# A graph-attention layer: the edge mask's chain started earlier, its merge moved to k steps 0 and 1, x loaded in whole rows, 12 more filler steps ahead of the scores

## The chip, the cores and the metric

One Trainium2 chip, one core. The metric is the device time of one execution in microseconds (us). The kernel before took 312.18 us (median of 3 runs, 310.19 to 312.44).

## The reference

There are 384 nodes with 1024 features, 16 heads of 64, and 6528 edges of the form (src, dst, type).

```python
h = jnp.maximum(_layernorm(x, axis=-1), 0.0)
q, k, v = h @ wq.T + bq, h @ wk.T + bk, h @ wv.T + bv
q2, k2, v2 = q @ wiq.T + biq, k @ wik.T + bik, v @ wiv.T + biv     # each split into 16 heads
w = softplus(edge_type_weights)
mask = full((384, 384), -inf); mask = mask.at[src, dst].set(w[edge_type - 1])
mask[i, i] = w[3] where the diagonal is still -inf
attn = softmax(q2 @ k2.T / 8 + mask)
out = x + (attn @ v2) @ wo.T + bo
```

Seven 1024x1024 weights are read, and the mask is a scatter of 6528 values into 384x384 cells, in which the last edge of a cell wins. All of it is in float32.

## The kernel before, in words

**Matmuls.** Each operand is split into a high and a low part in the matmul type fp32r (`split_hi`, L67, on ScalarE; `split_lo`, L79, on VectorE or GpSimd), and each product is three matmuls: high by high, high by low, low by high (L357 to L359). A weight comes in 8 chunks of 128x1024 (512 KB), loaded by SP (L65) into three `raw` buffers and split into four `whl` buffers.

**Stages.** The chunks are numbered w: 8 of v, 8 of q, 8 of v2 (`iv`), 8 of k, then 8 pairs of q2 and k2 (`iq`, `ik`), then 8 of the output. In the v, q and k stages (`proj`, L394) chunk m gives 128 rows of the transposed result in a PSUM bank `g`, 24 matmuls of 384 columns. At the head of each chunk (`slot_head`, L385) come the split of chunk w+2, the evacuation of the chunk before (`evac_row`, L370: L372 on VectorE scales by the row of 1/std and writes `f`, L373 on ScalarE makes the high part, L374 on VectorE the low one), and the load of chunk w+4. The order on every engine is the program's order, written by hand; every engine works strictly through it. The v2 stage (L492) has 18 matmuls of 512 columns a chunk and sums into six PSUM banks, one of them a `g` bank. They are evacuated one per chunk in the k stage (`v2_evac`, L503), the one in `g` last, so `g` has two banks for the k stage until then.

**Scores.** From L727 on, 48 steps (16 heads by 3 row tiles) do the scores, the softmax, the transposes and the product with v2. Between them a filler of q2/k2 chunks and then of output chunks is issued (`fill`, L712): `PRE` matmuls ahead of the first scores and `RATE` per step. Scores add the mask `ma` (L660).

**The mask.** `er` holds the edges with 128 per row, `ed` the same edges with 128 per column. `key_rows_a` and `key_rows_b` (L173, L177) make keys src*384+dst on GpSimd and write them to `krow` in DRAM; `key_load(g)` (L188) broadcasts a third of the rows to all partitions (3 DMAs of 384 KB). For each of 51 columns `mask_detect` (L204, VectorE) counts whether a later edge of the column has the same key; `mask_index` (L210) sends such edges to a dump cell. `mask_scatter` (L217) writes a column's 128 values by an indirect DMA from GpSimd into one of three DRAM tables in turn, so that the order between columns is kept by table; a scatter waits for the landing of the one before it in its table. The tables are cleared first (`table_clear`, L142, from `zero`). `val`, the softplus of the edge's type, is made on GpSimd after `softplus_c` (L160); `mask_base` (L197) puts the default on the diagonal of `ma`. At the end `mask_load` (L223) reads the three tables back and `mask_select` (L231, VectorE) merges each into `ma`, in order.

`detect(s)` (L419) places this in slots, one per chunk of v and q (s = 0 to 15): 5 detects a slot from s = 3, 3 scatters a slot from s = 7 and in each v2 chunk; `mask_load` stands at k step 2 and the merges at k steps 5, 6 and 7.

**The start.** x is loaded in six half tiles; statistics on VectorE (L243), the mean's subtraction on ScalarE, GpSimd and VectorE (`ln_sub`), transposes on TensorE (L284), high parts on ScalarE (L290), low parts on VectorE (L295). Then chunk 0's 24 matmuls (L402). `residual(k)` (L470), in the v2 stage, adds `bo` to x and keeps the sum in DRAM.

Of the kernel before, what the change touches and what calls it, by code (L numbers as in the profile page):

```python
# [8 lines left out]
F32 = mybir.dt.float32  # L9
# [3 lines left out]
OP = mybir.AluOpType  # L13
# [9 lines left out]
def gnn_kernel(ctx: ExitStack, tc: tile.TileContext, x, edges, erows, etw, wq, wk, wv, wiq, wik, wiv, wo,  # L23
# [15 lines left out]
    EB = 8  # L39
    DS = 3  # L40
    NTAB, RNG = 3, EC // 3
    WARM = (20, 0, 0, 0)

# [49 lines left out]
    for t in range(NT):  # L93
        for c in (slice(0, 512), slice(512, D)):
            nc.sync.dma_start(xt[t][:, c], x[t * 128:(t + 1) * 128, c])
    ert = work.tile([128, N], F32, tag="e", name="er", bufs=EB)
    er = ert[:EC, :256].bitcast(I32).rearrange("p (a j) -> p a j", a=2)
    nc.sync.dma_start(er, erows)
    load(0)
    ed = const.tile([128, 3 * EC], I32, name="ed")  # L100
# [5 lines left out]
    nc.sync.dma_start(ew, etw.partition_broadcast(128))  # L106
    load(2)
# [4 lines left out]
    nc.gpsimd.memset(upper, 1.0)  # L112
    nc.gpsimd.affine_select(upper, upper, pattern=[[1, 128]], compare_op=OP.is_gt, fill=0.0, base=0,
                            channel_multiplier=-1)
    epsc = const.tile([128, 1], F32, name="epsc")
# [17 lines left out]

    def mask_consts():
        nc.gpsimd.iota(dump.bitcast(I32), pattern=[[0, 1]], base=CELLS, channel_multiplier=1)
        nc.gpsimd.tensor_copy(w8[:, 8:9], dump.bitcast(I32))
        nc.gpsimd.memset(zero, 0.0)
        nc.gpsimd.memset(ma, -3.0e38)
        for j in range(NT):
            nc.gpsimd.tensor_scalar(ma[:, j, j * 128:(j + 1) * 128], ident, 3.0e38, -3.0e38, op0=OP.mult, op1=OP.add)  # L140
# [36 lines left out]
    def key_rows_b():  # L177
        nc.gpsimd.tensor_tensor(krt[:EC, :128], kf[:, 0, :], kf[:, 1, :], OP.add)
        nc.gpsimd.dma_start(krow, krt[:EC, :128])

# [6 lines left out]

    def key_load(g):  # L188
        t = work.tile([128, 2, NT, N], F32R, tag="pt", name="rows")
        rv = t.bitcast(F32).rearrange("p a k n -> p (a k n)")  # L190
        for s, (c0, c1) in enumerate(parts(g)):
            dst = rv[:, s * PA * 128:(s * PA + c1 - c0) * 128]
            for c in range(c0, c1):
                rows[c] = rv[:, (s * PA + c - c0) * 128:(s * PA + c - c0 + 1) * 128]
            nc.gpsimd.dma_start(dst, krow[c0:c1, :].rearrange("c j -> (c j)").partition_broadcast(128))

# [12 lines left out]

    def mask_index(cs):  # L210
        t0 = tmpe[:, 0, cs]
        nc.vector.tensor_scalar(t0, key[:, cs], -1.0, w8[:, 8:9], op0=OP.mult, op1=OP.add)
        nc.vector.scalar_tensor_tensor(t0, cnt[:, cs], 0.5, t0, op0=OP.is_gt, op1=OP.mult)
        nc.vector.tensor_tensor(t0, t0, key[:, cs], OP.add)
        nc.vector.tensor_copy(idx[:, cs], t0)

# [85 lines left out]

    mask_consts()
    warm(WARM[0])
    ln_bn(0, 0)
# [7 lines left out]
    p0 = ln_transpose(0)  # L313
    warm(WARM[1])
    ln_sub(1, 0, 512, nc.scalar)
    ln_sub(1, 512, D, nc.gpsimd)
    ln_hi(0, 0, p0[0])
    ln_bn(2, 0)
# [5 lines left out]
    p1 = ln_transpose(1)  # L324
    warm(WARM[2])
    ln_hi(1, 0, p1[0])
    ln_hi(1, 1, p1[1])
    p2 = ln_transpose(2)
    warm(WARM[3])
    t0 = wpool.tile([128, 2, D], F32R, tag="whl", name="whl", bufs=4)  # L330
    whl[0] = (t0[:, 0, :], t0[:, 1, :])
    for c in (slice(0, 512), slice(512, D)):
        nc.vector.tensor_copy(t0[:, 0, c], raw[0][:, c])
    for c in (slice(0, 512), slice(512, D)):
# [59 lines left out]
    def proj(src, dst, bidx, extra=None):  # L394
        nonlocal w
        for m in range(8):
            slot_head(w)
            ps = bank("g")
            if w == 0:
                for i, (a, b) in enumerate(((0, 0), (1, 0), (0, 1))):  # L400
                    for k in range(KT):
                        nc.tensor.matmul(ps[:, :N], whl[0][a][:, k * 128:(k + 1) * 128], src[:, b, k, :],  # L402
                                         start=(i == 0 and k == 0), stop=(i == 2 and k == KT - 1))
# [15 lines left out]
    def detect(s):  # L419

        if s == 0:
            softplus_a()
        if s == 1:
            softplus_b()
        if s == 2:
            softplus_c()
        if s == 2:
            key_load(1)
        if s == 3:
            mask_base()  # L430
        for i in range(max(5 * (s - DS), 0), max(0, min(EC, 5 * (s + 1 - DS)))):
            mask_detect(sc_order[i])
            if i % (NTAB * PA) == NTAB * PA - 1 or i == EC - 1:
                g = i // (NTAB * PA)
                for c0, c1 in parts(g):
                    mask_index(slice(c0, c1))
                if g == 0:
                    key_load(2)
        if s >= DS + 4:
            scatters(3)  # L440
        if s == DS + 11:
            biv_load()

# [48 lines left out]
    for k in range(8):  # L492
# [6 lines left out]
        scatters(3)  # L499
        residual(k)  # L500
        w += 1

    def v2_evac(i):  # L503
# [69 lines left out]
    LT, LA = 5, 7  # L573
    PRE, RATE, RATE_O, RATE_E = 72, 7.9, 8, 8
    WSTEPS = (37, 38, 41, 44, 47, 51)
# [239 lines left out]
```

## Time and profile before

| | us |
|---|---|
| median of 3 runs | 312.18 (310.19 to 312.44) |
| the profiled execution | 312.79 |
| its span, first to last instruction | 311.1 |
| first matmul of chunk 0 (L402) | 12.57 |
| first and last scatter start (L219) | 49.31, 136.56 |
| first merge (L233) | 143.41 |
| first scores (L654) | 168.54 |

The page shares out the span by engine: PE is TensorE's matmuls, PEld its weight loads, DVE VectorE, ACT ScalarE, POOL GpSimd, SP SyncE. Lists of waits name the waiting instruction, whom it waited for, the sum, the number and the longest. A row of the timeline has the start, the duration, engine, line, operation, output and inputs, and in brackets how long the engine sat idle before it and what ended that. Matmuls overlap: a row of 0.33 us follows the last by 0.17. PEclk is the TensorE clock that was granted, in tenths.

### The profile page before, as it was taken

The page shows a single profiled execution, that of the slowest core. Times are in us where ns is not written, and L with a number is a line of the kernel's source. Part 1 is how long each engine was busy: PE and PEld are TensorE (multiplying, and loading weights), DVE is VectorE, ACT ScalarE, POOL GpSimd, SP SyncE. Part 2 cuts the span into 40 slices and gives each one's busy share as a digit, 9 for nine tenths or more (in the row PEclk, how much of TensorE's full clock was granted, in tenths as well). Part 3 has the DMA queues.
Part 4 walks back from the last instruction along what each step waited for, and adds up shares of the span by engine and source line. Part 5 has one row for each costly group of instructions (what it writes and reads, how often), then busy time and mean ns, then how long its engine had stood idle before and what let it go on. Part 6 is the DMA issues. An engine that isn't in the chain of part 4 may idle for free.

```text
span 311.1 us, 4980 instructions
## 1 busy us (share of the span) xinstructions
PE 296.4 (95%) x1643; PEld 280.5 (90%) x1643; DVE 204.4 (66%) x519; ACT 154.2 (50%) x286; POOL 163.0 (52%) x172
## 2 busy tenths in 40 slices
PE   7899999999999999996995999999999999999995
PEld 5799999999888899995994899999999999888884
DVE  3976599999942436864961547576767676896413
ACT  2848242424632126432152477877768686876200
POOL 5655816568756655761033174655647388467010
PEclk9799999999999999998998899999999999999998
DMA  7697868635775776437249586464647477920005
GB/s 226 218 363 267 237 193 212 188 113 176 220 272 161 231 247 208 129 122 250 81 110 265 137 226 174 126 171 118 182 119 187 115 186 241 304 112 0 2 0 202
DMA packets 22031, 55.12 MB, mean 177 GB/s; under 512 B 4598, under 2 KB 8234, under 8 KB 22006
## 3 DMA queue, kind: packets, MB, share of 16 engines
q1 hardware_dynamic: 19190, 49.64, 51.5%
q0 software_dynamic: 2816, 5.17, 6.5%
q8 instruction: 13, 0.21, 0.3%
q14 instruction: 12, 0.10, 0.1%
HBM read 40.39 MB, written 4.97 MB: 146 GB/s over the span
## 4 chain that ended last, share of the span: by engine, by line
PE 45%; DMA 20%; DVE 19%; POOL 7%; issue 4%; ACT 3%; SPq 1%; DVEq 0%; ACTq 0%; POOLq 0%
DMA tab<-val,idx 11%; PE g L359 8%; PE g L357 8%; PE g L358 8%; DVE whl L82 6%; PE s L654 6%; PE a L691 5%; PE t L674 5%; POOL tab L219 5%; DVE junk L207 4%; DVE g L374 3%; DVE f L372 2%; DMA rows<-krow 2%; DMA krow<-kr 2%; DMA ks<-nat 2%
## 5 line engine op out<-in xcount | busy, mean ns | idle before, releaser
L357 PE MATMUL g<-g,whl 128*128 128x384 f32 x312 | 107.8, 346 | 3.1 <-DVE f L372 3.1
L359 PE MATMUL g<-g,whl 128*128 128x384 f32 x312 | 105.8, 339 | 0.4 <-DVE whl L82 0.4
L358 PE MATMUL g<-g,whl 128*128 128x384 f32 x312 | 105.5, 338 | 0.0
L219 POOL DMA_INDIRECT tab<-val,idx x51 | 58.3, 1143 | 30.2 <-DMA tab<-val,idx 16.5
L77 ACT ACTIVATE whl<-raw 128x1024 fp32r<-128x1024 f32 x51 | 53.4, 1051 | 35.6 <-DMA raw<-in_wk_dram 15.8
L669 POOL TENSOR_TENSOR e<-e,s 128x384 f32<-128x384 f32 x48 | 39.6, 828 | 46.7 <-DVE s L668 41.7
L357 PEld LDWEIGHTS g<-g,whl 128*128 128x128 f32 x312 | 59.5, 191 | 3.4 <-issue 3.4
L359 PEld LDWEIGHTS g<-g,whl 128*128 128x128 f32 x312 | 59.5, 191 | 0.7 <-DVE whl L82 0.7
L358 PEld LDWEIGHTS g<-g,whl 128*128 128x128 f32 x312 | 59.5, 191 | 0.0
L82 DVE TENSOR_TENSOR whl<-raw,whl 128x1024 fp32r<-128x1024 f32 x41 | 50.4, 1229 | 7.6 <-ACT whl L77 7.6
L373 ACT ACTIVATE g<-f,bc 128x384 fp32r<-128x384 f32 x24 | 14.8, 616 | 58.1 <-DVE f L372 48.8
L82 POOL TENSOR_TENSOR whl<-raw,whl 128x1024 fp32r<-128x1024 f32 x11 | 26.4, 2403 | 26.7 <-ACT whl L77 25.6
L664 ACT ACTIVATE e<-e,s 128x384 f32<-128x384 f32 x48 | 29.4, 612 | 15.5 <-DVE s L660 13.6
L684 DVE TENSOR_TENSOR pt<-t,pt 128x384 fp32r<-128x384 f32 x48 | 26.4, 550 | 7.7 <-ACT pt L683 7.0
L368 DVE SCALAR_TENSOR_TENSOR nat<-g,bc,nat 128x384 fp32r<-128x384 f32 x16 | 9.9, 618 | 29.7 <-ACT nat L367 27.3
L654 PE MATMUL s<-ks,qs 128*128 128x384 f32 x96 | 25.2, 343 | 4.2 <-DMA ks<-nat 3.6
L683 ACT ACTIVATE pt<-t 128x384 fp32r<-128x384 f32 x48 | 23.2, 483 | 10.1 <-PE t L674 9.6
L660 DVE CUSTOM_DVE_ANT_0 e<-s,ma 128x384 f32<-128x384 f32 x48 | 26.3, 549 | 2.8 <-PE s L654 2.5
L674 PE MATMUL t<-ident,e 128*128 128x128 f32 x144 | 23.5, 271 | 0.0
L654 PEld LDWEIGHTS s<-ks,qs 128*128 128x128 f32 x96 | 17.7, 191 | 5.5 <-issue 3.9
L674 PEld LDWEIGHTS t<-ident,e 128*128 128x128 f32 x144 | 18.8, 140 | 2.8
L691 PE MATMUL a<-pt,vhl 128*128 128x384 f32 x96 | 20.8, 351 | 0.0
(151 smaller groups left out, 422.1 us busy)
## 6 DMA issues: line engine op xcount, KB each, us to landing
ks<-nat SPq DMA_DIRECT2D x32, 192.0 KB
raw<-in_wv_dram SPq DMA_DIRECT2D x8, 512.0 KB
raw<-in_wq_dram SPq DMA_DIRECT2D x8, 512.0 KB
raw<-in_wiv_dram SPq DMA_DIRECT2D x8, 512.0 KB
raw<-in_wk_dram SPq DMA_DIRECT2D x8, 512.0 KB
raw<-in_wiq_dram SPq DMA_DIRECT2D x8, 512.0 KB
raw<-in_wik_dram SPq DMA_DIRECT2D x8, 512.0 KB
raw<-in_wo_dram SPq DMA_DIRECT2D x8, 512.0 KB
```

The costliest lines, as they stand in the source:

```text
L77: nc.scalar.activation(dst[0], raw[w], AF.Copy)
L82: (eng or nc.vector).tensor_tensor(lo, raw[w], hi.bitcast(F32), OP.subtract)
L219: nc.gpsimd.indirect_dma_start(out=tabs[c // RNG], out_offset=bass.IndirectOffsetOnAxis(ap=idx[:, c:c + 1], axis=0), in_=val[:, c:c + 1], ...
L357: nc.tensor.matmul(ps, lhi, rhi, start=first, stop=False)
L358: nc.tensor.matmul(ps, lhi, rlo, start=False, stop=False)
L359: nc.tensor.matmul(ps, llo, rhi, start=False, stop=last)
L654: nc.tensor.matmul(ps[:, :N], qs[:, o, t * 128:(t + 1) * 128], ks[:, o, s, :], start=(s == 0), stop=(s == 1))
L664: nc.scalar.activation(es[i], es[i], AF.Exp, bias=s[:, 0:1], scale=-1.0, accum_out=s[:, 1:2])
L669: nc.gpsimd.tensor_tensor(es[i], es[i], s[:, 2:3].to_broadcast([128, N]), OP.mult)
L674: nc.tensor.transpose(ps[:, k * 128:(k + 1) * 128], es[i][:, k * 128:(k + 1) * 128], ident)
L684: nc.vector.tensor_tensor(lo, pv, hi.bitcast(F32), OP.subtract)
L691: nc.tensor.matmul(ps[:, :N], vhl[:, k, p, 2 * o:2 * o + 2, :], pts[h][:, s, k, :], start=(k == 0 and s == 0), stop=(k == 2 and s == 1))
```

## The change

Key rows are made first on GpSimd; `er` is loaded from ScalarE's queue; `krow` and the key loads go by SP, spread over the slots. The constants of the mask follow the split of chunk 1. Detects begin at s = 2 (4 a slot behind the first), the index takes two operations per three columns of each table, scatters begin at s = 4, `mask_load` stands at v2 step 5 and the merges at k steps 0 (two) and 1. x is loaded in three whole tiles. Chunk 0's high part and the low part of v2 go from VectorE to GpSimd. In the filler the load leaves ahead of the split, and 84 matmuls stand ahead of the scores in place of 72, with 7.6 per step for 7.9.

```diff
-    DS = 3
+    DS, GI = 2, 3
     for t in range(NT):
-        for c in (slice(0, 512), slice(512, D)):
-            nc.sync.dma_start(xt[t][:, c], x[t * 128:(t + 1) * 128, c])
+        nc.sync.dma_start(xt[t], x[t * 128:(t + 1) * 128, :])
+    load(0)
...
-    nc.sync.dma_start(er, erows)
-    load(0)
+    nc.scalar.dma_start(er, erows)
...
-        nc.gpsimd.dma_start(krow, krt[:EC, :128])
+        nc.sync.dma_start(krow, krt[:EC, :128])
...
+    def key_load(g, s):
+        if s == 0:
+            t = work.tile([128, 2, NT, N], F32R, tag="pt", name="rows")
+            krv[g] = t.bitcast(F32).rearrange("p a k n -> p (a k n)")
+        c0, c1 = parts(g)[s]
...
+        nc.sync.dma_start(dst, krow[c0:c1, :].rearrange("c j -> (c j)").partition_broadcast(128))
...
-    def mask_index(cs):
-        t0 = tmpe[:, 0, cs]
-        nc.vector.tensor_scalar(t0, key[:, cs], -1.0, w8[:, 8:9], op0=OP.mult, op1=OP.add)
-        nc.vector.scalar_tensor_tensor(t0, cnt[:, cs], 0.5, t0, op0=OP.is_gt, op1=OP.mult)
-        nc.vector.tensor_tensor(t0, t0, key[:, cs], OP.add)
-        nc.vector.tensor_copy(idx[:, cs], t0)
+    def mask_index(j0, j1):
+        k, n, i, t0 = (a.rearrange("p (r j) -> p r j", r=NTAB)[:, :, j0:j1] for a in (key, cnt, idx, tmpe[:, 0, :]))
+        nc.vector.scalar_tensor_tensor(t0, n, 2.0 * CELLS, k, op0=OP.mult, op1=OP.add)
+        nc.vector.tensor_scalar(i, t0, w8[:, 8:9], None, op0=OP.min)
...
-    mask_consts()
-    warm(WARM[0])
+    warm(WARM)
+    key_rows_a()
+    key_rows_b()
+    load(2)
+    for s in range(NTAB):
+        key_load(0, s)
...
-        nc.vector.tensor_copy(t0[:, 0, c], raw[0][:, c])
+        nc.gpsimd.tensor_copy(t0[:, 0, c], raw[0][:, c])
...
     split(1, nc.gpsimd)
-    for g in range(NTAB):
-        table_clear(g)
-    key_rows_a()
-    key_rows_b()
-    key_load(0)
+    mask_consts()
     mask_keys()
+    mask_fill()
...
-        if s == 2:
-            key_load(1)
         if s == 3:
             mask_base()
-        for i in range(max(5 * (s - DS), 0), max(0, min(EC, 5 * (s + 1 - DS)))):
...
+        if s < NTAB:
+            table_clear(s)
+        if 3 <= s < 6:
+            key_load(1, s - 3)
+        if 7 <= s < 10:
+            key_load(2, s - 7)
+        if s == DS:
+            detects(5)
+        elif s > DS:
+            detects(4)
+        if s >= DS + 2:
+            scatters(3)
+        if s == DS + 12:
+            biv_load()
...
+    def detects(n):
+        for i in range(nde[0], min(EC, nde[0] + n)):
             mask_detect(sc_order[i])
+            if i % (NTAB * GI) == NTAB * GI - 1 or i == EC - 1:
+                mask_index(i // (NTAB * GI) * GI, i // NTAB + 1)
+            nde[0] = i + 1
...
         scatters(3)
         residual(k)
+        if k == 5:
+            mask_load()
...
-        nc.vector.tensor_tensor(vhl[:, t, h * 4:h * 4 + 4, 1:3, :], tv, hi.bitcast(F32), OP.subtract)
+        nc.gpsimd.tensor_tensor(vhl[:, t, h * 4:h * 4 + 4, 1:3, :], tv, hi.bitcast(F32), OP.subtract)
     def extra_k(m):
         if 0 < m <= 6:
             pend.append(lambda: v2_evac(m - 1))
-        if m == 2:
-            mask_load()
-        if m >= 5:
-            mask_select(m - 5)
+        for g in {0: (0, 1), 1: (2,)}.get(m, ()):
+            mask_select(g)
...
             for n in ("iq", "ik"):
+                load(w + 4)
                 split_hi(w + 2)
...
                 split_lo(w + 2, nc.gpsimd if (w + 2) % 2 == PAR else None)
-                load(w + 4)
...
-    PRE, RATE, RATE_O, RATE_E = 72, 7.9, 8, 8
+    PRE, RATE, RATE_O, RATE_E = 84, 7.6, 8, 8
```

More of the change, by code (lines that the diff above doesn't have):

```diff
@@ L39, in gnn_kernel @@
     EB = 8
-    DS = 3
+    DS, GI = 2, 3
     NTAB, RNG = 3, EC // 3
-    WARM = (20, 0, 0, 0)
+    WARM = 20
     def bank(tag):
@@ L106, in gnn_kernel @@
     nc.sync.dma_start(ew, etw.partition_broadcast(128))
-    load(2)
     ident = const.tile([128, 128], F32, name="ident")
@@ L111, in gnn_kernel @@
     upper = const.tile([128, 128], F32, name="upper")
-    nc.gpsimd.memset(upper, 1.0)
-    nc.gpsimd.affine_select(upper, upper, pattern=[[1, 128]], compare_op=OP.is_gt, fill=0.0, base=0,
-                            channel_multiplier=-1)
     epsc = const.tile([128, 1], F32, name="epsc")
@@ L134, in mask_consts @@
     def mask_consts():
+        nc.gpsimd.memset(upper, 1.0)
+        nc.gpsimd.affine_select(upper, upper, pattern=[[1, 128]], compare_op=OP.is_gt, fill=0.0, base=0,
+                                channel_multiplier=-1)
         nc.gpsimd.iota(dump.bitcast(I32), pattern=[[0, 1]], base=CELLS, channel_multiplier=1)
@@ L137, in mask_consts, with mask_fill @@
         nc.gpsimd.memset(zero, 0.0)
+    def mask_fill():
         nc.gpsimd.memset(ma, -3.0e38)
@@ L186, in parts @@
         return [(r * RNG + g * PA, min(r * RNG + (g + 1) * PA, (r + 1) * RNG)) for r in range(NTAB)]
[L188 to L195, printed above, removed]
+    krv = {}
+    def key_load(g, s):
[3 more added lines that the diff above has]
+        c0, c1 = parts(g)[s]
+        dst = krv[g][:, s * PA * 128:(s * PA + c1 - c0) * 128]
+        for c in range(c0, c1):
+            rows[c] = krv[g][:, (s * PA + c - c0) * 128:(s * PA + c - c0 + 1) * 128]
+        nc.sync.dma_start(dst, krow[c0:c1, :].rearrange("c j -> (c j)").partition_broadcast(128))
     def mask_base():
@@ L313, in gnn_kernel @@
     p0 = ln_transpose(0)
-    warm(WARM[1])
+    ln_hi(0, 0, p0[0])
     ln_sub(1, 0, 512, nc.scalar)
     ln_sub(1, 512, D, nc.gpsimd)
-    ln_hi(0, 0, p0[0])
     ln_bn(2, 0)
@@ L324, in gnn_kernel @@
     p1 = ln_transpose(1)
-    warm(WARM[2])
     ln_hi(1, 0, p1[0])
@@ L328, in gnn_kernel @@
     p2 = ln_transpose(2)
-    warm(WARM[3])
     t0 = wpool.tile([128, 2, D], F32R, tag="whl", name="whl", bufs=4)
@@ L399, in proj @@
             if w == 0:
-                for i, (a, b) in enumerate(((0, 0), (1, 0), (0, 1))):
-                    for k in range(KT):
+                for a, b, ks in ((0, 0, range(KT)), (1, 0, range(4)), (0, 1, range(4)), (1, 0, range(4, KT)),
+                                 (0, 1, range(4, KT))):
+                    for k in ks:
                         nc.tensor.matmul(ps[:, :N], whl[0][a][:, k * 128:(k + 1) * 128], src[:, b, k, :],
-                                         start=(i == 0 and k == 0), stop=(i == 2 and k == KT - 1))
+                                         start=(a == b == k == 0), stop=(b == 1 and k == KT - 1))
             else:
@@ L426, in detect @@
             softplus_c()
-        if s == 2:
-            key_load(1)
         if s == 3:
             mask_base()
-        for i in range(max(5 * (s - DS), 0), max(0, min(EC, 5 * (s + 1 - DS)))):
-            mask_detect(sc_order[i])
[L433 to L442, printed above, removed]
+        if s < NTAB:
[12 more added lines that the diff above has]
+            biv_load()
+    nde = [0]
+    def detects(n):
+        for i in range(nde[0], min(EC, nde[0] + n)):
+            mask_detect(sc_order[i])
+            if i % (NTAB * GI) == NTAB * GI - 1 or i == EC - 1:
+                mask_index(i // (NTAB * GI) * GI, i // NTAB + 1)
+            nde[0] = i + 1
     def extra_q(m):
```

## The prediction

> **What bounds the kernel now.** I read the busy table first, then who TensorE waited for, then TensorE and VectorE in order of time around the long waits, then GpSimd's scatters. Times are us from the start of the span; a slot is one weight chunk of 24 matmuls (18 in the v2 stage).
>
> The busy table and the granted clock:
>
> ```profile
> PE 296.4 (95%) x1643; PEld 280.5 (90%) x1643; DVE 204.4 (66%) x519; ACT 154.2 (50%) x286; POOL 163.0 (52%) x172
> ...
> PEclk9799999999999999998998899999999999999998
> ```
>
> TensorE is the bound: an edit counts only by what it does to TensorE's waits. There are few, so the view of TensorE's waits names nearly all that can be won:
>
> ```profile
> PE s L654 <- DMA ks<-nat: 3.6, 1, 3.6
> PE g L357 <- DVE f L372: 3.1, 1, 3.1
> PE s L284 <- ACT g L272: 2.1, 2, 1.4
> ```
>
> TensorE in order of time around the second of them:
>
> ```profile
> 142.02 0.34 PE L359 MATMUL g<-g,whl 128*128 128x384 f32 x1
> 145.43 0.49 PE L357 MATMUL g<-g,whl 128*128 128x384 f32 x1 [3.07 <-DVE f L372]
> 145.72 0.52 PE L358 MATMUL g<-g,whl 128*128 128x384 f32 x1
> 146.04 0.52 PE L359 MATMUL g<-g,whl 128*128 128x384 f32 x1
> ...
> 148.92 0.40 PE L359 MATMUL g<-g,whl 128*128 128x384 f32 x1
> 149.15 0.34 PE L357 MATMUL g<-g,whl 128*128 128x384 f32 x1
> ```
>
> Before it, matmuls start every 0.173 us. From 142.02 to 145.43 lies 3.41, so 3.24 are lost. Then they start every 0.32: twelve take 3.72 instead of 2.08, another 1.64. A stall costs twice: the windows view gives a granted clock of 0.53 for those 3.6 us, and 0.62 for the 4.46 us after the wait for ks (4.46 x 0.38 = 1.7).
>
> VectorE in the same place says what f was late for, and GpSimd in order of time says why:
>
> ```profile
> 143.41 1.44 DVE L233 COPY_PREDICATED ma<-mbs 128x1152 f32<-128x1152 int32 x1 [5.07 <-DMA mbs<-tab]
> 144.74 0.55 DVE L372 TENSOR_TENSOR f<-g,rrow 128x384 f32<-128x384 f32 x1
> ```
>
> ```profile
> 112.36 0.96 POOL L219 DMA_INDIRECT tab<-val,idx  x1 [0.30 <-issue]
> 114.41 1.17 POOL L219 DMA_INDIRECT tab<-val,idx  x1 [1.09 <-DMA tab<-val,idx]
> 119.30 0.96 POOL L219 DMA_INDIRECT tab<-val,idx  x1 [3.72 <-DMA tab<-val,idx]
> ...
> 136.56 0.96 POOL L219 DMA_INDIRECT tab<-val,idx  x1 [0.30 <-issue]
> 138.80 2.37 POOL L229 DMA_DIRECT2D mbs<-tab  x3 [1.28 <-DMA tab<-val,idx]
> ```
>
> The 51 scatters are written as three per slot but run at their own pace, first at 49.31, last at 136.56: 1.745 each. The first merge can start 6.85 after the last scatter starts (136.56 to 143.41), and VectorE, working in order, holds f of step 5 behind it. Step 7 of the k stage wants the PSUM bank of step 5 (the v2 sums hold the third bank). So the mask chain is the bound in this stage.
>
> **The change part by part.** The sum is made against the profiled execution: 312.79 us, span 311.1. It stands 0.6 above the median of the runs (312.18), so I take 0.6 off at the end.
>
> *Start.* The first real matmul is at 12.57. With whole rows bn_stats can't start at 3.40; the second half of tile 0 ended its wait at 4.59, and two bn_stats (0.69 each) and two small ones (0.36) then put the first subtraction at 6.3 instead of 5.75. But the wait for tile 1 (0.81, until 7.13) shrinks, and tile 2's statistics end at 9.55 instead of 9.70. Bounds: +0.6 (tile 0's delay carried through) and -0.7 (the 0.81 gone, less a little); I take -0.2, the chain just counted. ScalarE's first hi goes ahead of its second subtraction, into 1.82 of idle time: nothing. Chunk 0's hi goes from VectorE (2 x 0.42) to GpSimd: a half lies between the 128x153 cast (0.33) and the 512 subtraction (1.34), so both end between 10.1 and 12.1 after GpSimd's own 9.4, ahead of 12.57.
>
> *Key rows first, on GpSimd and SP.* Their source now leaves from ScalarE's queue with x at about 0.8; by the first half tile of x (0.80 to 3.40) it is there by 3.4. Then 0.40, 0.55 and 1.15 on GpSimd end at 5.6, before it is next needed (5.8). SP now waits for kr with load(2) behind it, which before left only at 7.78; then three row loads wait for krow, with load(3) behind them, which before left at 13.92, when its buffer came free. Before, krow took 7.1 from its issue to the loads' (19.47 to 26.57); from 5.7 that is 12.8: covered by 1.1, and with that gone ScalarE still reads the chunk only at 19.39. The table clears wait for zero, which now comes after split(1), at about 18; behind the first is load(5), which before left at 18.86. Nothing is charged. The constants (3.1 us of GpSimd) and the keys (1.9) move behind 16.94 and end by 22; val waits for w8 at 27.9 anyway.
>
> *Detection.* VectorE's nine index groups of four operations become six of two; five detects a slot become four. VectorE isn't the bound there: no TensorE wait lies between 19 and 142. Charged nothing.
>
> *Scatters.* They follow val and mask_base on GpSimd: 27.9, plus 4.2 for val (30.31 to 34.54), plus 4.0 for the diagonal (36.18 to 40.2), plus 0.3: first scatter at 36.4, 12.9 earlier. Indices are there by about 34. Then their pace, from windows of the same stages:
>
> ```profile
> 55.80:79.50 23.70, 16.98 (x15) 1.00 0.50 157
> 79.50:113.10 33.60, 21.91 (x20) 1.00 0.66 210
> 113.10:119.00 5.90, 1.39 (x2) 1.00 0.94 346
> 119.00:137.60 18.60, 14.33 (x13) 1.00 0.41 136
> ```
>
> The columns are the stretch, GpSimd's busy time in scatters (and their number), the clock, the DMA share and GB/s. From start to start it is 1.64 in the q stage (55.82 to 78.73, 14 steps), 1.77 in v2 (78.73 to 112.36, 19 steps), about 1.5 scatters in all in the 6.2 us across the end of v2, and 1.44 behind it (119.30 to 136.56, 12 steps). Moved there: 36.4 to 79.3 gives 26.2 (number 27.2); v2 gives 19.0 (46.2 at 112.9); 47.7 by 119.1; the last 3.3 take 4.8: number 51 starts at 123.8. Unseen is the pace in the v stage, beside key loads that now come from SP. Bounds: 1.44 and the 2.17 of the first four scatters (49.31 to 55.82, beside row loads); I take 1.64, the neighbouring stretch, since VectorE has fewer detects a slot and the queue more loads.
>
> *Merge at k steps 0 and 1.* The first merge starts at 123.8 + 6.85 = 130.7. Two now stand in front of f of step 0. Before, merge start to TensorE was 2.02 (143.41 to 145.43); one merge more is 1.46: TensorE gets its bank at 134.2. The k stage's first matmul was at 113.05, so step 2 needs it at 113.05 + 2 x 4.16 - 0.2 = 121.2. **New stall: 13.0, and 1.65 for the clock behind it.** Held behind the merge on VectorE are f, the low halves of the weights and so SP's next load; all catch up at 2.9 + 1.5 per slot of 4.16, so I charge them nothing more.
>
> *What goes.* The stall at 142 (3.24 + 1.65) and the one at the first scores (3.79 + 1.65): 10.33. The latter because VectorE no longer merges at steps 5 to 7 (f of step 7 came at 155.84, 4.6 after TensorE had ended that step at 151.2) and because 12 more matmuls (2.08) stand before the scores. Before, scores were wanted 13.5 after the k stage's end and ks landed at 17.3; now wanted at 15.6, landing between 12.7 (all of the 4.6 gone) and 17.3: a rest between 0 and 1.7, I take 0.5. The rate falls so that the filler still ends after 39.5 steps (300/7.6, before 312/7.9): no gain in the tail. In the q2/k2 filler each load goes out ahead of the split and of the stack copies: its buffer came free a chunk (4.16) earlier, so it holds up nobody: nothing. The v2 subtraction on GpSimd (six, each near the 1.34 of its 512 subtraction) is first read near 189: hidden.
>
> **Sum:** -0.2 - 10.33 + 0.5 + 13.0 + 1.65 = +4.6: 317.4 for the profiled execution, **316.8** on the median.
>
> Two rules against this. The rows: within 79.5 to 119.5 GpSimd waited eight times, 12.5 us, for an earlier scatter of the same table; two took 7.4 from issue to landing. The Trainium skill, DMA: Bandwidth & Descriptors, "Anatomy of one DMA — SWDGE (gpsimd) path", gives a fixed cost of about 2 us. By it three tables would hide every landing, the pace would be an estimated 1.45, the mask on time and the sum 302.2; the measured 12.5 us decides. The other way: scatters lasted 0.96 at least and 1.85 at most, mean 1.18 in the q stage. The Trainium skill, GPSIMD Engine Reference, "Specifications", says GpSimd shares its SBUF interfaces with VectorE and contends with instructions of two SBUF inputs, which the splits and detects are. Were every scatter of v and q stretched to 1.85, the estimate would be 326; the mean says one in four.
>
> **The rivals.**
> *A, the mask is in time (faster).* One mechanism: GpSimd's pace. The first merge must start by 121.2 - 2.02 - 1.46 = 117.7, so number 51 by 110.9: 1.49 per scatter from 36.4. For it: 1.44 between 119 and 137. Against: 1.64 and 1.77 in the two stages that the scatters mostly cross. Then 312.79 - 0.2 - 10.33 + 0.5 - 0.6 = 302.2. Faster and slower part at a stall of 8.4: 51 at 119.2, 1.66 per scatter, where mine is 1.75.
> *B, half late.* 1.60 to 1.68 per scatter: number 51 at 116.4 to 120.4, stall 5.6 to 9.6, 309 to 313.5.
> *C, later still.* 1.9 in v and q (half way to 2.17): number 51 at 129.0, 322. Or ks is late as before and the clock falls again: 1.2 + 1.65 more, 319.7.
>
> **How the numbers follow.** My forecast (313.5 to 320 by itself) 0.50, A 0.20, B 0.20, C 0.10. Range 305 to 321.5: it leaves out most of A and the top of C. One per cent, 3.1 us, is about what a measurement of this kernel can tell from no change. Faster (below 309.1): A and a little of B, 0.24. Within (to 315.3): most of B, the lower edge of the forecast, 0.24. Slower: 0.52.
>
> **What would show it.** Right: first scatter near 36, last near 124; one wait of VectorE for mbs of over 10 us from about 115; a TensorE gap near 121 ending on f, a clock near 0.5 behind it; no gap before the first scores. Wrong: a last scatter before 111, or VectorE merging without a wait; a gap at the scores of over 2 us; a first matmul after 13.2.

## The result, and the profile after

The changed kernel took **321.26 us** (median of 6 runs, 320.11 to 322.48); the kernel before took 313.03 (6 runs, the three from before the change among them, 310.19 to 314.72). Ratio 1.0265, 95% interval 1.0206 to 1.0324: slower, as forecast, but by 8.2 us where the prediction had 4.6. The profiled execution took 321.02 (span 319.3). Times and ratios here are of fast executions, except where a run has only one; now and then a kernel runs in a slower state, some per cent longer, as e12_pre120 did when it was profiled (328.0).

| us from the span's start | before | after |
|---|---|---|
| first matmul of chunk 0 | 12.57 | 14.14 |
| first matmul of the k stage | 113.05 | 113.85 |
| first, last scatter start | 49.31, 136.56 | 39.09, 122.92 |
| first merge start | 143.41 | 128.28 |
| first scores | 168.54 | 174.91 |
| last scores | 278.55 | 286.71 |
| end | 311.09 | 319.31 |

The busy table of after and its clock. TensorE's busy time is what it was (296.7, before 296.4); the span grew. So nearly all of the 8.2 us is time in which TensorE had nothing to do.

```profile
PE 296.7 (93%) x1643; PEld 279.9 (88%) x1643; DVE 202.4 (63%) x487; ACT 153.8 (48%) x286; POOL 167.2 (52%) x170
...
PEclk9999999999999999599999999999999999999999
```

TensorE's longest waits in after: one of 9.9 where 3.1 stood, no wait for ks any more, and five waits of scores for VectorE (5.0 in all), where before had one of 0.55.

```profile
PE g L358 <- DVE f L373: 9.9, 1, 9.9
PE s L665 <- DVE s L671: 5.0, 5, 1.6
PE s L287 <- ACT g L275: 2.6, 2, 2.2
```

The first of them, TensorE in order of time. It stops in k step 2 and misses 10.04 us (132.23 minus 122.02 minus 0.173); then matmuls start every 0.32 again.

```profile
122.02 0.34 PE L360 MATMUL g<-g,whl 128*128 128x384 f32 x1
132.23 0.66 PE L358 MATMUL g<-g,whl 128*128 128x384 f32 x1 [9.87 <-DVE f L373]
132.69 0.52 PE L359 MATMUL g<-g,whl 128*128 128x384 f32 x1
133.01 0.52 PE L360 MATMUL g<-g,whl 128*128 128x384 f32 x1
```

VectorE at that time: it stands at the first merge for 12.27 us, with f behind two merges.

```profile
128.28 1.43 DVE L236 COPY_PREDICATED ma<-mbs 128x1152 f32<-128x1152 int32 x1 [12.27 <-DMA mbs<-tab]
130.21 1.43 DVE L236 COPY_PREDICATED ma<-mbs 128x1152 f32<-128x1152 int32 x1 [0.51 <-DMA mbs<-tab]
131.54 0.54 DVE L373 TENSOR_TENSOR f<-g,rrow 128x384 f32<-128x384 f32 x1
```

GpSimd behind it: the end of the 51 scatters and the load of the tables. The merge starts 5.36 after the last scatter starts.

```profile
120.39 0.96 POOL L222 DMA_INDIRECT tab<-val,idx  x1 [1.02 <-DMA tab<-val,idx]
121.65 0.96 POOL L222 DMA_INDIRECT tab<-val,idx  x1 [0.30 <-issue]
122.92 0.96 POOL L222 DMA_INDIRECT tab<-val,idx  x1 [0.30 <-issue]
123.88 2.37 POOL L232 DMA_DIRECT2D mbs<-tab  x3
```

The third of the five waits, VectorE and then TensorE in order of time. The filler chunk's sum is ready, VectorE evacuates it (`nat`), makes a weight's low half behind it (L82, 1.21), and only then adds the mask to the scores of the step before (L671). Two banks `s` hold scores, so the next scores wait.

```profile
190.65 0.62 DVE L369 SCALAR_TENSOR_TENSOR nat<-g,bc,nat 128x384 fp32r<-128x384 f32 x1 [2.72 <-ACT nat L368]
191.19 1.21 DVE L82 TENSOR_TENSOR whl<-raw,whl 128x1024 fp32r<-128x1024 f32 x1
192.32 0.55 DVE L671 CUSTOM_DVE_ANT_0 e<-s,ma 128x384 f32<-128x384 f32 x1
```

```profile
190.98 0.34 PE L360 MATMUL g<-g,whl 128*128 128x384 f32 x1
192.93 0.62 PE L665 MATMUL s<-ks,qs 128*128 128x384 f32 x2 [1.61 <-DVE s L671]
```

By stage, after minus before: to the first matmul of k +0.80; from there to the first scores 61.06 for 55.49, +5.57; to the last scores 111.80 for 110.01, +1.79; behind them +0.06. The third term looks small and is not. A fall was due there: 12 matmuls fewer (2.08) and no slowed clock (1.65).

### The profile page after: what moved, and what is told of

Its sections match the earlier page's. It is cut to its first block, busy times and chain, and to the rows that moved or that the text cites. A ratio compares the mean times of both kernels' runs of the same rounds, so it can differ in the third digit from the quotient of the medians.

```text
span 319.3 us, 4955 instructions
## 1 busy us (share of the span) xinstructions
PE 296.7 (93%) x1643; PEld 279.9 (88%) x1643; DVE 202.4 (63%) x487; ACT 153.8 (48%) x286; POOL 167.2 (52%) x170
## 3 DMA queue, kind: packets, MB, share of 16 engines
HBM read 40.39 MB, written 4.97 MB: 142 GB/s over the span
## 4 chain that ended last, share of the span: by engine, by line
PE 66%; DMA 16%; POOL 5%; issue 5%; DVE 4%; ACT 2%; SPq 0%; POOLq 0%; DVEq 0%
PE g L358 16%; PE g L360 16%; PE g L359 16%; DMA tab<-val,idx 12%; PE a L702 5%; PE s L665 5%; PE t L685 5%; POOL tab L222 4%; DMA mbs<-tab 2%; DMA g<-in_x_dram 1%; DVE whl L82 1%; PE g L404 1%; DMA qs<-nat 1%; ACT nat L368 1%; DVE lnt L246 1%
## 5 line engine op out<-in xcount | busy, mean ns | idle before, releaser
L222 POOL DMA_INDIRECT tab<-val,idx x51 | 56.8, 1114 | 28.3 <-DMA tab<-val,idx 13.5
L358 PEld LDWEIGHTS g<-g,whl 128*128 128x128 f32 x312 | 59.3, 190 | 10.2 <-issue 10.2
L82 DVE TENSOR_TENSOR whl<-raw,whl 128x1024 fp32r<-128x1024 f32 x41 | 50.0, 1219 | 9.1 <-ACT whl L77 9.1
L675 ACT ACTIVATE e<-e,s 128x384 f32<-128x384 f32 x48 | 29.4, 612 | 13.5 <-DVE s L671 13.3
L82 POOL TENSOR_TENSOR whl<-raw,whl 128x1024 fp32r<-128x1024 f32 x11 | 27.1, 2463 | 15.1 <-ACT whl L77 13.6
L671 DVE CUSTOM_DVE_ANT_0 e<-s,ma 128x384 f32<-128x384 f32 x48 | 26.2, 548 | 1.1 <-PE s L665 0.9
L375 DVE SCALAR_TENSOR_TENSOR g<-f,bc,g 128x384 fp32r<-128x384 f32 x24 | 21.1, 884 | 0.7 <-ACT g L374 0.7
L524 POOL TENSOR_TENSOR vhl<-tv,vhl 128x512 fp32r<-128x512 f32 x6 | 9.2, 1537 | 23.3 <-ACT vhl L523 23.3
```

Of the source, the lines that this page charges most:

```text
L82: (eng or nc.vector).tensor_tensor(lo, raw[w], hi.bitcast(F32), OP.subtract)
L222: nc.gpsimd.indirect_dma_start(out=tabs[c // RNG], out_offset=bass.IndirectOffsetOnAxis(ap=idx[:, c:c + 1], axis=0), in_=val[:, c:c + 1], ...
L358: nc.tensor.matmul(ps, lhi, rhi, start=first, stop=False)
L671: nc.vector.tensor_tensor_reduce(e, st_ps.pop(i)[:, :N], ma[:, t, :], -0.125, 3.0e38, OP.add, OP.min, s[:, 0:1])
L675: nc.scalar.activation(es[i], es[i], AF.Exp, bias=s[:, 0:1], scale=-1.0, accum_out=s[:, 1:2])
```

## The experiments

Theories: **M**, the stall in the k stage is the merges standing at steps 0 and 1 ahead of a late mask. **P**, the waits in the scores come from the place in a step at which a filler chunk ends: `PRE` 84 is 3.5 chunks, `PRE` 72 is three. **T**, the scatters are slow because their landings queue behind other DMA traffic of the v2 stage. **X**, whole rows of x delay the start. Rivals are named with each run. In kernels with x in halves the line numbers are one higher. The profile of each run is of one execution.

### e1_merge567: the merges alone back at steps 5 to 7

```diff
-        for g in {0: (0, 1), 1: (2,)}.get(m, ()):
-            mask_select(g)
+        if m >= 5:
+            mask_select(m - 5)
```

> The changed kernel with the three merges put back to k steps 5, 6 and 7 (the mask is still loaded at v2 step 5). Theory M (the merges at steps 0 and 1 wait for a mask that lands near 128, and VectorE holds the k stage behind them): the TensorE gap of 10.0 us near 122 and the 2.1 us of slow clock behind it go, VectorE waits for no mask, last scatter still near 123; time about 321.3 - 12.2 = 309, up to 312.5 if the merges again delay the stacks and TensorE waits at the first scores (3.3 and 1.65 for the clock). Rival W (weights, or the v2 evacuation that now goes over GpSimd, hold the k stage): a TensorE gap stays in the k stage and the time stays over 317.

Measured: ratio 0.9977 (0.9931 to 1.0023), span 309.1. No gap in the k stage; the merges start at 138.56, 143.75 and 148.94 without a wait; the last scatter is at 122.9, as in after. TensorE's waits:

```profile
PE s L665 <- DVE s L671: 5.0, 5, 1.6
PE s L287 <- ACT g L275: 2.4, 2, 1.9
PE s L665 <- DMA ks<-nat: 1.7, 1, 1.7
```

M holds: 10.2 us of span go. The wait for ks, absent in after, is back with 1.7: the stall had hidden it. The five waits for VectorE stay to the tenth, so they have nothing to do with the mask.

### e2_merge567_halves: the same with x in six half tiles

```diff
-        nc.sync.dma_start(xt[t], x[t * 128:(t + 1) * 128, :])
+        for c in (slice(0, 512), slice(512, D)):
+            nc.sync.dma_start(xt[t][:, c], x[t * 128:(t + 1) * 128, c])
```

> As the run with the merges at k steps 5 to 7, and x loaded in six half tiles as before. Theory X (whole rows make the first statistics wait for the whole of tile 0, 5.60 for 3.40): first matmul of chunk 0 back from 14.1 to 12.6 to 13.1, 1.0 to 1.5 us less time than that run. Rival E (the edge rows loaded beside x, or chunk 0's high part on GpSimd, hold the start): first matmul stays at 14.0 or later, time the same within 0.3.

Measured: ratio 0.9985 (0.9918 to 1.0053), span 309.1: no time is won, where X expected 1.0 to 1.5. The first matmul comes at 12.83 (e1 13.90), the k stage at 112.68 (113.76), but the wait for ks is 3.1 (1.7): what the start won was waited for later. X is only made likely: the first matmul came at 13.2 to 14.1 in eight of nine profiles with whole rows and at 11.61 in one, and at 12.5 to 13.4 in five with halves and the new order. Two profiles of the kernel before's own start have 12.57 and 11.14. That spread is as large as the difference. Nor is E out: the first statistics start at 4.72 to 5.60 in the nine and at 4.50 to 4.83 in the five, but at 3.40 and 3.47 with the kernel before's own start. So something else in the new order, such as the edge rows beside x, also delays them; no run takes it apart.

### e3_pre72: after with the filler's old numbers

```diff
-    PRE, RATE, RATE_O, RATE_E = 84, 7.6, 8, 8
+    PRE, RATE, RATE_O, RATE_E = 72, 7.9, 8, 8
```

> The changed kernel with 72 matmuls ahead of the scores and 7.9 a step, as before. Theory P (where in a step a filler chunk ends sets whether the next scores wait for VectorE; 84 puts the end in the second half of a step, 72 at its beginning): the five TensorE gaps between 178 and 240, 5.0 us, go; at the first scores TensorE waits for ks, 0 to 2 us, and if it is long enough the clock falls (1.65); time 316 to 319. Rival L (the load that leaves ahead of the split and of the stack copies is what is late): the gaps stay, time 321 to 323.

Measured: 316.74 and 316.32, two executions and so no ratio; span 315.0, 4.3 under after, though its stall in the k stage is 1.2 longer. TensorE's waits:

```profile
PE g L358 <- DVE f L373: 11.1, 1, 11.1
...
PE s L665 <- DVE s L671: 0.6, 1, 0.6
```

Five waits of 5.0 became one of 0.6: P holds. No wait for ks, although the 12 matmuls ahead of it are gone.

### e4_loadlast: after with the filler's load behind the split

```diff
-                load(w + 4)
                 split_hi(w + 2)
...
                 split_lo(w + 2, nc.gpsimd if (w + 2) % 2 == PAR else None)
+                load(w + 4)
```

> The changed kernel with the filler's load back behind the split and the stack copies. Theory P (the place of a chunk's end in a step): the gaps between 178 and 240 stay, time 321 within 0.5. Rival L (the early load): the gaps go, time near 316.

Measured: ratio 1.046 (1.0411 to 1.0509), span 321.9. The rival L, that the early load makes the new waits, falls: without it they are longer. P's time (321 within 0.5) fails too: 325.41. The first of the five waits grows from 1.0 to 3.5, and the clock is halved behind it. TensorE's waits:

```profile
PE g L358 <- DVE f L373: 8.7, 1, 8.7
PE s L665 <- DVE s L671: 7.4, 5, 3.5
```

### e5_pre72: e2_merge567_halves with the filler's old numbers

The edits of e1, e2 and e3 together.

> The kernel after with the merges at k steps 5, 6 and 7, x in six half tiles, and 72 matmuls ahead of the scores with 7.9 per step: the run e2_merge567_halves with the filler's old phase alone. Theory P (the 5.0 us of waits in five gaps of the scores come from where in a step a filler chunk ends): the five gaps go (under 1.2 left), the wait of the first scores for ks grows by the 2.1 that twelve matmuls cover, from 3.4 to 5.5; span 309.1 - 4 + 2.1 - 0 to 1.5 = 305 to 307.5. Rival Q (the gaps come from the earlier load or from VectorE's other work in the scores, not from the phase): the gaps stay at 4 to 5 and the span is 310 to 312.

Measured: ratio 0.9847 (0.9774 to 0.992), span 303.3, 5.8 under e2; the profiled execution is the fastest of e5, and the medians, 308.23 and 311.18, lie 3.0 apart. TensorE's waits:

```profile
PE s L666 <- DMA ks<-nat: 3.0, 1, 3.0
...
PE s L666 <- DVE s L672: 0.6, 1, 0.6
```

P holds a second time. But the wait for ks did not grow by 2.1; it is 3.0 for 3.1. Twelve more matmuls ahead of the scores covered nothing of that wait here: ks landed 2 us later with them (164.84 for 162.54, k stages 0.3 apart). Why was not settled.

### e6_pre96: merges at steps 3 to 5, halves, 96 matmuls ahead and 8 per step

```diff
-        for g in {0: (0, 1), 1: (2,)}.get(m, ()):
-            mask_select(g)
+        if 3 <= m < 6:
+            mask_select(m - 3)
...
-    PRE, RATE, RATE_O, RATE_E = 84, 7.6, 8, 8
+    PRE, RATE, RATE_O, RATE_E = 96, 8, 8, 8
```

> The kernel after with the merges at k steps 3, 4 and 5, x in six half tiles, and 96 matmuls ahead of the scores with 8 per step (exactly three steps per chunk, a chunk always ending at the start of a step). Theories M and P together: no stall in the k stage over 2 (the mask lands by about 128 to 129.5, the first merge is due near 128), no gaps in the scores over 1.2 in sum, and 24 more matmuls (4.1 us) than 72 ahead of the scores cover the wait for ks to 1.5 or less: span 301 to 304.5, ratio 0.965 to 0.98. Rival Q (the scores' gaps do not come from the phase): 4 to 5 us more, 306 to 309.

Measured: ratio 0.9772 (0.9691 to 0.9853), span 305.6: between M with P (up to 304.5) and Q (from 306), so the span does not decide. The waits do: scores waited for VectorE 0.5 in all, where Q had 4 to 5. What M with P missed is in the k stage: two waits for f (1.5), since the first merge started at 129.70 and the second only at 136.04. The wait for ks is 1.0.

### e7_before84: the kernel before with the filler's new numbers alone

```diff
-    PRE, RATE, RATE_O, RATE_E = 72, 7.9, 8, 8
+    PRE, RATE, RATE_O, RATE_E = 84, 7.6, 8, 8
```

> The kernel before with nothing changed but 84 matmuls ahead of the scores and 7.6 per step. Theory P: the wait for ks (3.6) shrinks by the 2.1 of twelve matmuls, and some 4 to 5 us of gaps on VectorE appear in the scores: 312 to 315.5, ratio 1.0 to 1.01. Rival (twelve more matmuls ahead of the scores are a plain gain, as the prediction charged them): no new gaps, 308.5 to 311, ratio 0.99 to 0.995.

Measured: ratio 1.0239 (1.0147 to 1.033), span 318.5, 7.4 over before. TensorE's waits:

```profile
PE s L654 <- DVE s L660: 8.7, 5, 4.8
PE g L357 <- DVE f L372: 4.1, 1, 4.1
...
PE s L654 <- DMA ks<-nat: 1.0, 1, 1.0
```

One line of numbers costs the kernel before nearly what the whole change costs it. P was right in kind and too low in size: the waits are 8.7, not 4 to 5. The first is 4.8; before's load stands behind the split, and e4, with the load there, has 3.5 in that place where after has 1.0. The sum: 8.2 more of such waits (8.7 for 0.55), 1.0 more at f, 2.6 less at ks, 2.1 for the 12 matmuls ahead of the scores, 1.1 less behind them (2.1 of work, less what the restarts cost besides the waits), and a k stage that began 0.2 earlier: 7.4.

### e11_rate8: after with 84 matmuls ahead and 8 per step

```diff
-    PRE, RATE, RATE_O, RATE_E = 84, 7.6, 8, 8
+    PRE, RATE, RATE_O, RATE_E = 84, 8, 8, 8
```

> The kernel after with 84 matmuls ahead of the scores as it has, but 8 per step in place of 7.6: a filler chunk is then exactly three steps long, and every chunk ends in the second half of a step. Theory P (the place in a step where a chunk ends makes the wait): waits of scores for VectorE at most of the chunk ends, 8 to 16 us in sum where the kernel after has 5.0; span 322 to 330. Rival (only the first few chunk ends after the start of the scores are hurt, whatever their place): 3 to 6 us of waits, span 317 to 320.

Measured: 326.72 (one execution), span 325.0. Scores waited for VectorE six times, 4.5 in all: half of P's lower bound, and within the sum that the rival gave. They follow the matmuls at 178.87, 191.81, 207.38, 222.95, 238.51 and 254.08, every six steps, so at every second chunk. VectorE in order of time at one chunk end and the next:

```profile
190.59 0.62 DVE L369 SCALAR_TENSOR_TENSOR nat<-g,bc,nat 128x384 fp32r<-128x384 f32 x1 [2.35 <-ACT nat L368]
191.12 1.22 DVE L82 TENSOR_TENSOR whl<-raw,whl 128x1024 fp32r<-128x1024 f32 x1
192.25 0.55 DVE L671 CUSTOM_DVE_ANT_0 e<-s,ma 128x384 f32<-128x384 f32 x1
...
198.88 0.62 DVE L369 SCALAR_TENSOR_TENSOR nat<-g,bc,nat 128x384 fp32r<-128x384 f32 x1 [3.35 <-ACT nat L368]
199.42 0.55 DVE L671 CUSTOM_DVE_ANT_0 e<-s,ma 128x384 f32<-128x384 f32 x1
```

At 191.12 VectorE makes the low half (1.22) ahead of L671; at 199.42 it does not, since GpSimd has that chunk's, and nothing waits. So here it takes both: a chunk end late in the step, and VectorE's split behind it. In after, four of the five waits have that split in front of L671; the shortest (0.46, ended at 184.80) has none: VectorE evacuates at 183.66 and goes on to L671 at 184.19. The rival, that only the first chunks are hurt, falls: the waits recur to 254. The span is 5.7 longer than in after. Of that, 0.8 is a longer stall for f (10.6), 2.6 are two waits for e on GpSimd near the end, and 1.7 is the slowed clock behind these; why they came stays open.

### e10_best and e12_pre120: e6 with the merges at 5 to 7, and with 120 ahead

```diff
-        if 3 <= m < 6:
-            mask_select(m - 3)
+        if m >= 5:
+            mask_select(m - 5)
...
-    PRE, RATE, RATE_O, RATE_E = 96, 8, 8, 8
+    PRE, RATE, RATE_O, RATE_E = 120, 8, 8, 8
```

The second edit is that of e12_pre120 alone.

> The kernel after with merges at k steps 5, 6 and 7, x in six half tiles, 96 matmuls ahead of the scores and 8 per step. Theories M and P: no gap in the k stage, none over 1 in the scores; the wait for ks is between 0.5 and 2.5, since the run e6_pre96 had lost 1.2 in the k stage that helped to cover it. Span 302 to 305, ratio 0.962 to 0.98. Rival: the gaps of the scores come back (4 to 5): 307 to 310.

Measured: ratio 0.9834 (0.9715 to 0.9953), span 304.5. TensorE's waits:

```profile
...
PE t L686 <- POOL e L681: 1.4, 1, 1.4
PE s L666 <- DVE s L672: 0.9, 1, 0.9
PE s L666 <- issue: 0.3, 1, 0.3
```

Nothing is left at ks or in the k stage. The wait of 1.4 for e, over the limit of 1, was not expected. It and e5 and e6 beat the kernel before by 1.5 to 2.3%, each with an interval below 1; the intervals overlap, so none of the three is the best.

> The run e10_best with 120 matmuls ahead of the scores (five whole chunks) in place of 96. Theory P: no waits of scores for VectorE over 1, no wait for ks; the filler ends three steps earlier, so some steps at its end have less to do: span 300 to 305. Rival (the tail grows by what the start wins, or the copies of the stacks wait for buffers): span 304 to 309.

Measured: ratio 1.0334 (1.0206 to 1.0462): P's expectation fails. Only the kind of the waits is read from its profile. Scores waited for VectorE nine times, 13.6 in all. ScalarE's rows say why for one of these (3.35):

```profile
177.22 0.58 ACT L369 ACTIVATE nat<-g,bc 128x384 fp32r<-128x384 f32 x1 [2.12 <-DMA ks<-nat]
177.70 0.60 ACT L676 ACTIVATE e<-e,s 128x384 f32<-128x384 f32 x1
```

The evacuation waits for one of the two `nat` buffers, which the copies into ks had not yet left. ScalarE stood before this line for such copies (into qs and ks) nine times, 22.5 in all, where e10 has one such wait of 3.5. The rival (copies wait for buffers) fits. The chunks end at the start of a step here as in e6 and e10, so the place in the step is not the only thing that makes such waits, and more matmuls ahead is no plain gain.

### e8_nores, e9_resk, e13_noadd, e14_nostore: what makes the scatters slow

`residual(k)` loads x, adds bo, and stores, in the v2 stage: 12 transfers of 256 KB, 3 MB. e8 drops it, e9 moves it to the k stage, e13 drops its additions, e14 its stores; so e8, e13 and e14 leave the addition of bo out. These three have one execution each.

The first edit is e8_nores. e9_resk has its first line too; in place of the other two it calls `residual(m)` in the k stage, and its merges stand as in e1:

```diff
-        residual(k)
...
-            nc.sync.dma_start(xb[t], xbd[t * 128:(t + 1) * 128, :])
+            nc.sync.dma_start(xb[t], x[t * 128:(t + 1) * 128, :])
```

e13_noadd takes out the first of these lines, e14_nostore the second (and reads `xb` from x as e8 does):

```diff
-                nc.vector.tensor_tensor(xh[i], xh[i], xh["b"][:, c], OP.add)
...
-                nc.sync.dma_start(xbd[r, c], xh[i])
```

> The kernel after without the sum of x and bo in the v2 stage and its traffic (the output stage adds x alone, so adding bo is left out). Theory T (the scatters' pace in the v2 stage is set by landings that queue behind other DMA traffic): the last scatter starts at 117 to 120, the stall in the k stage falls to 6 to 8. Rival (the pace is GpSimd's own, or that of the weight loads): last scatter 121 to 123, stall 9 to 10.5 as in the kernel after.

> The kernel after with the sum of x and bo (its loads, adds and stores) moved from the v2 stage to the k stage, nothing left out; merges at k steps 0 and 1 as in the kernel after. Theory T (this traffic is what slows the scatters of the v2 stage): the last scatter starts at 114 to 117 where the kernel after has 122.9, the wait of VectorE for mbs falls below 8, TensorE's stall in the k stage to 3 to 6; span 310 to 314. If the adds and the evacuations of v2 now collide in the k stage, up to 2 us more. Rival (the run without the sum gained for another reason): last scatter 121 to 123, stall 9 to 10.5, span 318 to 320.

> The kernel after with the loads and stores of the sum of x and bo as they are, but without VectorE's six additions (adding bo is left out). Theory T (the DMA traffic slows the scatters): 18 or 19 scatters between 81 and 114, last scatter 121 to 124, stall 9 to 10.5, as in the kernel after. Rival (VectorE's additions, sharing something with GpSimd, slow them): 22 to 23 scatters there, last scatter 114 to 117, stall 3 to 6.

> The kernel after with the loads and the additions as they are, but without the stores of the sum (the output stage adds x alone, so adding bo is left out). Theory T, with the slowing in proportion to the bytes: half of the traffic's effect, 20 or 21 scatters between 81 and 114, last scatter 117 to 120, stall 5.5 to 8. If only the stores do it: 22 to 23 scatters, last one 114 to 116. Rival (the additions do it): 18 scatters, last one 121 to 124.

The expectation of e9 describes it wrongly in one point: its merges stand at steps 5 to 7. What it says of the stall at steps 0 and 1 thus can't be read from it; its scatters can.

Scatters by stretch, after first, then e8, e9, e13 and e14. The columns are the stretch, GpSimd's busy time in scatters (their number), the clock, the DMA share and GB/s:

```profile
81.00:114.00 33.00, 19.99 (x18) 1.00 0.67 215
```

```profile
81.00:114.00 33.00, 22.83 (x23) 1.00 0.47 145
```

```profile
81.00:114.00 33.00, 22.10 (x23) 1.00 0.53 168
```

```profile
81.00:114.00 33.00, 19.52 (x17) 1.00 0.69 211
```

```profile
81.00:114.00 33.00, 22.72 (x20) 1.00 0.65 211
```

| | last scatter | stall in k (start to start) | span |
|---|---|---|---|
| after | 122.92 | 10.21 | 319.3 |
| e8, no sum | 113.78 | 3.70 | 309.4 |
| e9, sum in k | 114.71 | (other merges) | 333.7 |
| e13, traffic alone | 125.36 | 12.50 | 322.1 |
| e14, without stores | 120.03 | 6.93 | 315.8 |

T holds in that this traffic sets the pace, more strongly than expected in e8 and as expected in e9 (114 to 117). From the 25th scatter, ahead of the first load of the sum (79.30 in after), to the 51st it took 46.5 in after, 38.8 in e8 and 38.7 in e9. The traffic alone (e13) leaves the scatters slower than after has them, a little beyond the expected 121 to 124; VectorE's additions don't set the pace. The time that GpSimd waited for an earlier scatter of the same table goes with it: 13.5 in after, 7.1 in e8, 6.0 in e9, 18.3 in e13. That the landings queue behind the bulk transfers is the likely reason; no run shows the queue itself.

Without the stores (e14) the last scatter comes 2.9 earlier, at the late edge of the expectation. But in the ten profiles of the new order with the whole sum untouched it lies between 121.16 and 124.20, so e14 is only 1.1 outside that spread, and two weight chunks more fell into its stretch (211 GB/s as in e13): what the stores alone do stays open.

e8's first matmul was also 2.5 earlier, by the spread named above, and with it the k stage (111.32) and its end; so up to 2.5 of the 9.9 in the span is that. Its scatters began as in after (38.89 for 39.09), but 1.5 of the 9.1 by which the last is earlier were there by the 25th (74.95 for 76.46), which the sum of x and bo doesn't explain.

e9 shows where the traffic can't go. VectorE in order of time:

```profile
128.46 0.69 DVE L520 TENSOR_TENSOR tv<-s,bivt 128x512 f32<-128x512 f32 x1 [5.68 <-DMA xbd<-xh]
...
132.36 0.55 DVE L373 TENSOR_TENSOR f<-g,rrow 128x384 f32<-128x384 f32 x1
```

The evacuation of v2 now waits for the buffers (`nat`) that the stores still read, five times, 21.3 in all, with f behind it; TensorE waited 16.3 for f, and the ratio is 1.0645 (1.051 to 1.0781): the expected span of 310 to 314, with at most 2 us for this collision, fails.

## Why the prediction was right or wrong

- **The mechanism and the sign: right.** The mask lands after k step 2 needs its bank, VectorE holds f behind two merges, and the new stall is worth more than the two that go. e1 shows it: with the merges back at steps 5 to 7 the 10.2 us are gone.
- **"New stall: 13.0, and 1.65 for the clock behind it": mis-sized, too high by 2.5.** Measured 10.04, and 2.1 for the clock (that much later than at 0.173 a matmul the work behind it ends). The first scatter was 2.7 late (39.09 for 36.4: `val` began at 29.34 instead of 27.9 and took 5.3 instead of 4.2), but the pace was 1.68 where 1.75 was taken, so the last came 0.9 early (122.92); the merge followed it by 5.36 instead of 6.85; the bank was due at 122.2 instead of 121.2, since the start was late. The second merge waited 0.51 for its own table, which was not foreseen.
- **The pace of the v2 stage: right for a reason that was not stated.** 1.77 was taken from the rows of before, and 1.78 was measured. The share of traffic was beside it in the same rows (0.66) and was not read: the sum of x and bo, which the change leaves where it is, sets that pace (e8, e9, e13). The rule weighed there (the Trainium skill, DMA: Bandwidth & Descriptors, "Anatomy of one DMA — SWDGE (gpsimd) path") gives about 2 us fixed. In that stretch of after a scatter took 4.4 us (median) from issue to landing, so the measurement was the right one to go by. Without the sum's traffic the scatters of e8 start every 1.53, close to the estimated 1.45.
- **What goes, 10.33: right.** Both waits are gone (TensorE's list), and with them 1.65 of slowed clock at each. The "rest" of 0.5 at the scores was 0. That the 12 matmuls cover the wait for ks is not so: e2 and e5 differ by them and wait 3.1 and 3.0. In after the stall itself hid it: without it, 1.7 came back (e1). "No TensorE wait lies between 19 and 142" overlooked one of 0.38 at 51.48, for a weight's low half; after does not have it.
- **The start, -0.2: wrong, +0.8 at the k stage** (+1.57 at the first matmul). The whole tile was taken to land when its second half had, at 4.59; the first statistics waited until 5.60, and the first subtraction came at 7.35, not at 6.3. The prediction's own sign of being wrong, "a first matmul after 13.2", came (14.14). How much of it is the whole rows, how much the rest of the new order and how much the spread from run to run stays open.
- **"The filler still ends after 39.5 steps: no gain in the tail": the step that failed most, 5.5 too low.** The prediction looked at when the filler ends and not at where in a step its chunks end. Five waits of scores for VectorE (4.97 for 0.55 before) came of it, as e3, e5 and e7 show: 4.4. The other 1.1 is what their restarts cost. From the last matmul ahead of a wait to the first filler matmul behind it, which lie 0.52 apart where nothing waits, the five took 6.34 longer (4.97 of it listed as waits), the one of before 0.82: 5.5 in all. "No gap before the first scores" did hold; nothing was said of gaps behind them.
- **The filler's early load, "holds up nobody: nothing": wrong the other way.** e4 shows 2.4 us fewer waits of scores with it (5.0 for 7.4). It is not charged in the sum below, since it is inside the 5.5.

The sum, term by term, measured minus predicted: start +1.0, stall and clock -2.5, rest -0.5, scores +5.5; together +3.5. The prediction had +4.6, and +8.2 was measured (0.1 is rounding and the end). That it came as near as this is luck in part: 3.0 too high and 6.5 too low stand against each other.

Rival A needed the last scatter by 110.9; even without the sum of x and bo it came at 113.78 with a stall of 3.4. Rival C's time (322) was near, by another way than C's.

## What to carry to other kernels

A number that spreads filler over the steps of a pipeline moves where each filler chunk ends in its step, and with that what an engine that works in order does ahead of the next step's release: change it only with the order written out at the chunk's ends, above all when nothing else seems to depend on it. Where a chain of small transfers is late, look at what bulk traffic stands beside it and whether that can wait, before moving the chain's end. And moving a consumer earlier is only worth as much as its producer is early: compare the moved due time with the landing, wait by wait.

## What the runs showed of the hardware

TensorE's clock behind the stop cost more than the prediction had it. The windows of after, around the stall; the columns are the stretch, busy time (number) of each engine, the granted clock, the DMA share and GB/s:

```profile
122.10:132.23 10.13, 0.26 (x2) 0.03 (x1) 3.45 (x4) 0.11 (x1) 3.83 (x5) 0.71 0.53 175
132.23:136.60 4.37, 4.37 (x14) 4.37 (x15) 4.37 (x6) 2.39 (x4) 0.00 (x0) 0.50 0.36 120
136.60:140.00 3.40, 3.40 (x21) 3.40 (x20) 3.40 (x5) 1.81 (x3) 1.54 (x1) 1.00 0.41 153
```

After 10 us without work the clock was 0.50 for 4.4 us of work, where 3.4 us without work had cost 0.53 for 3.6. The loss does not go by the length of the stop alone. In after the half clock was granted from about 126.4, inside the stop, to 136.6; the work lost time only in what of this lay behind the restart. A stop of 9.1 (start to start) in e4 lost 2.65, one of 10.2 in after 2.1, one of 3.7 in e8 1.4, and those of 3.4 for ks in e2 and e5 lost nothing: the clock behind them was 1.00. So "a stall costs twice" held for both stalls of the kernel before, and not for every stall of that length.

An indirect scatter of one column, about 1.1 us of GpSimd's time (means of 1.06 to 1.19 between 81 and 114 in before, after, e7, e8, e11, e13 and e14), came every 1.52 and 1.53 us without the 3 MB of bulk traffic in that stage (e9, e8) and every 1.69 to 1.99 with it (13 profiles).
